# A graph layer on one core: VectorE's work kept behind each turning of edges, and more source rows fetched singly by SyncE

## The chip, the cores and the metric

The kernel runs on one core of a Trainium2 chip. The core has five engines that run at the same time, each with its own in-order queue: TensorE (PE; its weight loads are listed as PEld), VectorE (DVE), ScalarE (ACT), GpSimd (POOL) and SyncE (SP). Sixteen DMA engines move the data that these queues ask for. The metric is the time of one execution on the device in microseconds.

## The reference

One layer of a graph network on 8192 nodes with 256 channels and 131072 edges, sorted by their target node, all in float32:

```python
ea = edge_attr @ w_e + b_e                      # 131072 x 64 @ 64 x 256
msg = relu(x[src] + ea)                         # gather of source rows
agg = segment_sum(msg, dst, num_segments=8192)
t = x + agg
h_local = bn(relu(t @ w1 + b1) @ w2 + b2 + x)
# dense attention inside graphs of 32 nodes, 4 heads
h_attn = bn(attention(x) @ out_w.T + out_b + x)
out = h_local + h_attn
out = bn(out + relu(out @ m_w1 + m_b1) @ m_w2 + m_b2)
result = layernorm(x + out)
```

## The kernel before, in words

The edges are cut into 128 blocks of 1024. For each block:

- GpSimd gathers 1024 source rows into the tile xs by eight indirect DMAs of 128 rows (`gather`, L217). There are six xs buffers. Block 20 and later gather from xb, a copy of x with a bias added, that SyncE writes early on.
- SyncE loads the edge features of a pair of blocks into the tile ea by four DMAs of 256 KB (`load_edges`, L268). There are two ea buffers, a pair each.
- VectorE turns a block's features (`edge_transpose`, L288, a STREAM_TRANSPOSE eaT<-ea); there are two eaT buffers.
- TensorE multiplies them by the weights (`edge_products`, pe<-we,eaT). L174 is the line of a helper that issues nearly all matmuls.
- VectorE adds the products to the gathered rows (`edge_messages`, L348, xs<-pe,xs) and ScalarE takes the relu (L352).
- TensorE sums the messages by target (pw<-xs,oh, with oh built by VectorE's compares at L363), and later places the sums among the nodes of a chunk (l<-oh, and VectorE's xT<-l at L422).

Beside this runs all other work for sixteen chunks of 512 nodes: attention, then the dense layers. A chunk begins with the load of its nodes by ScalarE's queue (`load_nodes`, L428, xn<-in_x_dram, 512 KB) and ends with a store by SyncE (L749). In attention ScalarE copies the scores from PSUM (pr<-pe, L629) and VectorE turns them (bd<-pr, L649).

TensorE's order is written out by hand; VectorE's and ScalarE's too up to block 24 (NV). From there on a scheduler orders these two, with `tc.issue_after` keeping messages (L330) and compares (L359) behind the last turn. From block 104 (TAIL) on a planner sets the order, with `came` as the times at which blocks' rows are expected. GpSimd's gathers are held in step by `hold_fetches`: gather number n waits for a TensorE instruction of the written order whose modelled time is n × 1.254 − 10.

For the blocks in FETCHED the last of the eight gathers is left out, and SyncE fetches these 128 rows one by one into the tile xf (`row_stream`, L235 to L243): a step is one TENSOR_LOAD of sixteen addresses into SyncE's registers and sixteen DMAs of 1 KB, and eight steps make a block. `fetch_rows(b)` adds RUN to a quota for every block from FROM on; `some_rows` issues one step if the quota is 1 or more. It is called by `between()`, which is called after a block's messages. Their messages are three additions instead of one (L342): three quarters of the last pair from xs in two pieces, and the last quarter from xf.

SyncE's edge loads, rows and stores and ScalarE's xn loads share eight completion semaphores, handed out in turn in the order of the program. Each of these DMAs stands in its queue until the one that had its semaphore before has landed. So the rows behind four edge loads come to stand on them, and once per chunk a row of SyncE stands on ScalarE's xn load.

Of the kernel before, what the change touches and what calls it, by code (L numbers as in the profile page):

```python
# [12 lines left out]
AF = mybir.ActivationFunctionType  # L13
ALU = mybir.AluOpType
# [5 lines left out]
P = 128  # L20
N, C, E, ED, H, NPG = 8192, 256, 131072, 64, 4, 32
# [3 lines left out]
NB = E // BE  # L25
NH = 4
WN = P // NH
TJ = BE // NH // P
TB = NH * TJ
QR = 32  # L30
EQ = P // QR
# [7 lines left out]
GT = P // NPG  # L39
NX = 20  # L40
BUFS = 6
RUN = 0.75
RL = 4
FETCHED = [44, 54, 64, 76, 86, 98]
FROM = 26
ND = 2
NV = 24
TAIL = 104
# [36 lines left out]
def gnn_kernel(ctx: ExitStack, tc: tile.TileContext, x, src, dst, edge_attr, w, out):  # L85
    nc = tc.nc
# [16 lines left out]
    iota_n = const.tile([P, WB], FP, name="iota_n")  # L103
# [15 lines left out]
    rel = const.tile([P, NB, TB], FP, name="rel")  # L119
# [13 lines left out]
    r = 0  # L133
    for v in VECS:
        n = w[v].shape[0] // P
# [53 lines left out]
    def hold_fetches():  # L189
# [3 lines left out]
        for n, fetch in fetches:  # L193
# [8 lines left out]
            if i:  # L202
# [2 lines left out]
                    mybir.DependencyInfo(mybir.DependencyClass.Sync, mybir.DependencyReason.DATA), reason="hold",  # L205
                )

    def gather(b):
        xs = epool.tile([P, NH, TJ, C], FP, name="xs", tag="xs", bufs=BUFS)
        for h in range(NH):  # L210
            for j in range(TJ):
                if b in FETCHED and h * TJ + j == TB - 1:
                    continue
                idx = srcd[:, b * NH + h, j : j + 1] if b < ND else srci[:, b, h * TJ + j : h * TJ + j + 1]
                fetches.append((
                    b * TB + h * TJ + j,
                    nc.gpsimd.indirect_dma_start(  # L217
                        out=xs[:, h, j, :],
                        out_offset=None,
                        in_=x if b < NX else xb[:, :],  # L220
                        in_offset=bass.IndirectOffsetOnAxis(ap=idx, axis=0),
                    ).ins,
                ))
        xs_of[b] = xs

    last_src = const.tile([P, P], I32, name="last_src")
    xb_bytes = xb.rearrange("(o n) c -> o (n c)", o=1).bitcast(U8)
    xf_of = {}

    def row_stream():  # L230

        for b in FETCHED:
            xf = xf_of[b] = epool.tile([P, C], FP, name="xf", tag="xf", bufs=2)
            for r in range(0, QR, RL):
                _, rows = nc.values_load_multi_w_load_instructions(  # L235
                    last_src[b : b + 1, r * EQ : (r + RL) * EQ], engines=[mybir.EngineType.SP],
                    min_val=0, max_val=(N - 1) * C * 4,
                    skip_runtime_bounds_check_because="src holds rows of x, as for the gathers",
                )
                for i, at in enumerate(rows):  # L240
                    p = i % EQ * QR + r + i // EQ
                    nc.sync.dma_start(xf[p : p + 1, :].bitcast(U8), xb_bytes[:, ds(at, C * 4)])
                yield  # L243

    rows_to_come = row_stream()
# [2 lines left out]
    def fetch_rows(b):  # L248
        quota[0] += RUN if b >= FROM else 0

# [7 lines left out]
    def load_edges(b, n=2):  # L258
# [6 lines left out]
        for j in range(TJ):  # L265
            for i in range(ED // QR):
# [4 lines left out]
                )  # L271

    gather(0)
    gather(1)

    eaT_of, spots = {}, []
    stated = [True]

    def between():
        for do in spots:  # L280
            do()

    turned_at = [None]

    def edge_transpose(b):
        ea, g0 = ea_of[b // 2], b % 2 * NH * EQ
        eaT = eaT_of[b] = epool.tile([P, NH * EQ, QR], FP, name="eaT", tag="eaT", bufs=2)
        turned_at[0] = nc.vector.transpose(eaT, ea[:, QR:].rearrange("p (g d) -> p g d", d=ED)[:, g0 : g0 + NH * EQ, :QR]).ins  # L288


    pe_of, msg_of, oh_of, pw_of, newest = {}, {}, {}, {}, {}
# [30 lines left out]
    def edge_messages(b, pairs=range(0, NH, 2), of_pair=range(2)):  # L322

        xs = xs_of[b]
        if b not in msg_of:
            msg_of[b] = xs
        msg = msg_of[b]
        n = 2 if b < NB - 1 else 1
        with ExitStack() as behind:
            if not stated[0]:  # L330
                behind.enter_context(tc.issue_after(turned_at[0]))
            for h in pairs:
                pe = pe_of[b, h]
                for u in of_pair[::n]:
                    hs = slice(h + u, h + u + n)
                    if h + u + n == NH and b in FETCHED:
                        for us, js, rows in (
                            (slice(0, 2), slice(0, TJ - 1), xs[:, h:]), (slice(0, 1), slice(TJ - 1, TJ), xs[:, h:]),
                            (slice(1, 2), slice(TJ - 1, TJ), xf_of[b]),
                        ):  # L340
                            rows = rows[:, None, None, :] if rows is xf_of[b] else rows[:, us, js].rearrange("p u i c -> p i u c")
                            nc.vector.tensor_add(  # L342
                                msg[:, h:][:, us, js].rearrange("p u i c -> p i u c"), pe[:, js, us, :], rows
                            )
                        nc.scalar.activation(msg[:, hs], msg[:, hs], AF.Relu)
                        continue
                    for js in [slice(0, TJ)] if n == 2 or h + u < NH - 1 else [slice(j, j + 1) for j in range(TJ)]:
                        nc.vector.tensor_add(  # L348
                            msg[:, hs, js].rearrange("p u i c -> p i u c"), pe[:, js, u : u + n, :],
                            xs[:, hs, js].rearrange("p u i c -> p i u c"),  # L350
                        )
                        nc.scalar.activation(msg[:, hs, js], msg[:, hs, js], AF.Relu)  # L352
        between()

    def edge_hot(b):

        oh = oh_of[b] = epool.tile([P, TB, WN], FP, name="oh", tag="oh", bufs=2)
        with ExitStack() as behind:
            if not stated[0]:  # L359
                behind.enter_context(tc.issue_after(turned_at[0]))  # L360
            for t0 in range(0, TB, TB // 2):
                ts = slice(t0, t0 + TB // 2)
                nc.vector.tensor_tensor(  # L363
                    oh[:, ts],
                    iota_n[:, None, :WN].to_broadcast([P, TB // 2, WN]),
                    rel[:, b, ts, None].to_broadcast([P, TB // 2, WN]),
                    ALU.is_equal,
                )

    def group_sums(pw, i, b, turns):  # L370
        for h, j in turns:
# [58 lines left out]
    with tc.tile_pool(name="setup", bufs=1) as sp:  # L430
# [16 lines left out]
        for v in VECS:  # L447
            r, n = col[v]
# [14 lines left out]
        for b in range(2):  # L463
            edge_transpose(b)
            load_edges(b + 2)
# [86 lines left out]
        for h in range(1, NH):  # L552
            step = sp.tile([P, 1], FP, name="step", tag="step", bufs=2)
            nc.vector.tensor_scalar(step, iota_p, float(h * WN), float(-WN), ALU.is_ge, ALU.mult)
            nc.vector.tensor_add(iota_w, iota_w, step)
# [298 lines left out]
    class Work:  # L854
# [41 lines left out]
        def step(self, t, until):  # L896

            n = len(self.streams)
            for i in [k % n for k in range(self.turn, self.turn + n)]:
                while self.streams[i] and self.streams[i][0][0]() and t >= self.at[i]:  # L900
                    d = next(self.streams[i][0][1], None)
                    if d is None:
                        self.streams[i].pop(0)
                        self.at[i] = max(self.at[i], self.placed_at)
                    elif d == REST:
                        self.at[i] = t + 6.0
                    elif d > 0:
                        t += d
                        self.at[i], self.turn = t + 0.5, (i + 1) % n
                        return t  # L910
            later = [a for a, q in zip(self.at, self.streams) if q and q[0][0]() and a > t]
            return min([until, *later])
# [11 lines left out]
    with tc.manual_schedule(engines={PE}):  # L924
# [39 lines left out]
        for i, c, a, z in (  # L964
# [4 lines left out]
            if c < NCH - 1:  # L969
                d = dense(c * CH, chunk[c], npool, bank, a, z, *own)  # L970
            elif z < CH:
                d = dense_rows(c * CH, chunk[c], npool, bank, a, *own)
            else:
                d = last_part = dense_rows(c * CH, chunk[c], npool, lambda: next(last_banks), a, ahead=True)
# [10 lines left out]
        b = 0  # L985
        while b < TAIL:
# [24 lines left out]
            if stated[0]:  # L1011
# [8 lines left out]
                if waiting:  # L1020
                    pair_sums(1, waiting)
                    sums = edge_sums(waiting)
                waiting = list(blocks)
                edge_hot(b)
                edge_products(b + 1)
                edge_messages(b + 1)
# [32 lines left out]
            copy_some(4 * TN)  # L1059
            b += 2  # L1060

        came = [8.7 + 10.035 * (i + 1) for i in range(NB)]
        t, l, s = came[b - 2] + 20, b - 2, b - 2
        p, m = [b, 0], [b, 0]
        added = dict((i, came[i] + 2.0) for i in range(b))
# [9 lines left out]
        while l < NB:  # L1075
# [56 lines left out]
            elif t >= times[2]:  # L1132
                i, k = p
# [17 lines left out]
    with tc.If(wide > 0):  # L1151
        with tc.tile_pool(name="gen", bufs=1) as pool, tc.tile_pool(name="gen_ps", bufs=1, space=PSUM) as ps_pool:
# [11 lines left out]
            with tc.For_i(0, E, P * TE) as e0:  # L1164
                ea = pool.tile([P, TE, ED], FP, name="gea")
# [7 lines left out]
                xs = pool.tile([P, TE, C], FP, name="gxs")  # L1173
# [7 lines left out]
                for j in range(TE):  # L1181
# [4 lines left out]
                    pe = ps_pool.tile([P, C], FP, name="gpe", bufs=2)  # L1186
                    nc.tensor.matmul(pe, et, we[:ED, :], start=True, stop=True)
                    msg = pool.tile([P, C], FP, name="gmsg", bufs=2)
                    nc.vector.tensor_add(msg, pe, xs[:, j, :])
                    nc.scalar.activation(msg, msg, AF.Relu)  # L1190
                    d = df[:, j : j + 1]
# [79 lines left out]
```

## Time and profile before

| what | value |
|---|---|
| median of 3 runs | 1311.12 us (1310.87 to 1316.0) |
| profiled execution | 1310.63 us, span 1308.9 us |
| mean granted TensorE clock | 0.966 |
| gathers on GpSimd | 1018 |
| row DMAs on SyncE | 768, in 48 steps |
| edge loads on SyncE | 252 of 256 KB, 8 of 128 KB |
| VectorE's messages at L348 | 253 additions, 300.0 us |

The span is the time between the first and the last instruction that the profile has; the execution's own time is 1.73 us longer. All rows of the trace are in microseconds from the span's start. In a timeline's row the first number is the start, the second the time that the group of like instructions took, with their gaps; behind the operation stand output and inputs by the program's names, then how many there are, and in square brackets the idle time ahead of it and what ended it. SPq and ACTq are the queues in which SyncE and ScalarE issue DMAs.

### The profile page before, as it was taken

Reading aid. Unit: us, or ns where it says so; the run is one execution under the profiler, and the core shown is the slowest. Engines: PE = TensorE matmul, PEld = TensorE weight load, DVE = VectorE, ACT = ScalarE, POOL = GpSimd, SP = SyncE. Lnnn points to the kernel's source line nnn. Section 1 sums busy time; section 2 is a strip of 40 time slices with the busy share of each in tenths; the row PEclk is TensorE's granted clock in tenths of the full one; section 3 lists DMA queues with packets and bytes.
Section 4 is the critical chain, followed back from the end, with each engine's and each line's share of the span. In section 5 each row is a group of like instructions: output and inputs, shape, how many; then the busy total and the mean of one; then the engine's idle time right before and its main releaser. Section 6 shows DMA issues by size and latency. Waiting matters only on the chain.

```text
span 1308.9 us, 23368 instructions
## 1 busy us (share of the span) xinstructions
PE 1200.1 (92%) x7671; PEld 722.8 (55%) x7671; DVE 792.5 (61%) x1643; ACT 581.6 (44%) x840; POOL 971.1 (74%) x1026
## 2 busy tenths in 40 slices
PE   4997999899979989798998979979889999999997
PEld 3564556555546545555555545545455655556576
DVE  6676856647446565474746638346565765666563
ACT  3443534445526354352544426425245544545343
POOL 6777777777777777777777777777777777777772
PEclk9998999999999989899999989989989999999999
DMA  8999987767768657667687765866777775777642
GB/s 235 290 298 331 285 218 171 166 174 172 187 151 202 155 152 183 163 159 184 155 187 182 175 167 145 190 162 175 183 186 170 189 182 138 202 160 183 150 133 62
DMA packets 146298, 240.53 MB, mean 184 GB/s; under 512 B 24606, under 2 KB 109756, under 8 KB 145404
## 3 DMA queue, kind: packets, MB, share of 16 engines
q0 software_dynamic: 48864, 133.50, 38.1%
q1 hardware_dynamic: 88828, 98.15, 32.4%
q10 hardware_dynamic: 8480, 7.35, 1.9%
q8 instruction: 62, 1.02, 0.3%
q14 instruction: 64, 0.52, 0.1%
HBM read 222.13 MB, written 16.78 MB: 183 GB/s over the span
## 4 chain that ended last, share of the span: by engine, by line
PE 76%; DMA 9%; issue 5%; DVE 4%; POOL 3%; ACT 1%; SPq 0%; DVEq 0%; POOLq 0%; ACTq 0%
PE at L174 38%; PE pe L174 20%; PE pw L174 9%; PE l L174 5%; DMA xs<-xb,srci 4%; POOL xs L217 3%; DVE xs L348 2%; DMA xn<-in_x_dram 2%; DMA xs<-in_x_dram,srci 1%; PE at L775 1%; PE at L178 1%; DMA ea<-in_edge_attr_dram 1%; PE at L726 1%; ACT xs L352 1%; DMA last_src<-in_src_dram 0%
## 5 line engine op out<-in xcount | busy, mean ns | idle before, releaser
L217 POOL DMA_INDIRECT xs<-xb,srci x858 | 815.4, 950 | 262.3 <-issue 181.4
L352 ACT ACTIVATE xs<-xs 128x1024 f32<-128x1024 f32 (+2 forms) x253 | 263.0, 1045 | 434.0 <-DVE xs L348 357.8
L348 DVE TENSOR_TENSOR xs<-pe,xs 128x1024 f32<-128x1024 f32 (+2 forms) x253 | 300.0, 1204 | 211.1 <-PE pe L174 105.4
L174 PE MATMUL pe<-we,eaT 64*128 64x256 f32 x2048 | 271.1, 401 | 10.1 <-DVE xs L348 8.7
L174 PEld LDWEIGHTS pe<-we,eaT 64*128 64x128 f32 x2048 | 196.1, 194 | 108.5 <-issue 66.3
L174 PE MATMUL pw<-xs,oh 128*32 128x256 f32 x2048 | 142.9, 395 | 32.4 <-issue 20.2
L217 POOL DMA_INDIRECT xs<-in_x_dram,srci x144 | 138.6, 962 | 45.2 <-issue 29.3
L174 PEld LDWEIGHTS pw<-xs,oh 128*32 128x32 f32 x2048 | 61.0, 111 | 113.7 <-issue 54.1
L174 PE MATMUL at<-xT,inT 128*128 128x512 f32 x256 | 121.2, 600 | 1.9 <-ACT xT L578 1.9
L174 PE MATMUL at<-hA,mw 128*128 128x512 f32 (+1 forms) x256 | 114.4, 573 | 0.0
L288 DVE STREAM_TRANSPOSE eaT<-ea 128x512 f32<-128x512 f32 x128 | 89.6, 701 | 36.2 <-PE pe L174 31.4
L174 PE MATMUL at<-m,mw 128*128 128x512 f32 (+1 forms) x256 | 108.9, 570 | 0.0
L174 PEld LDWEIGHTS l<-oh,ws 128*128 128x128 f32 x512 | 74.7, 197 | 20.3 <-issue 16.4
L422 DVE TENSOR_TENSOR xT<-l,xT 128x352 f32<-128x352 f32 (+14 forms) x107 | 43.2, 427 | 70.4 <-PE l L174 70.3
L174 PE MATMUL l<-oh,ws 128*128 128x160 f32 (+4 forms) x512 | 85.8, 308 | 0.0
L174 PEld LDWEIGHTS at<-xT,inT 128*128 128x128 f32 x256 | 47.0, 190 | 60.5 <-issue 50.5
L174 PEld LDWEIGHTS at<-m,mw 128*128 128x128 f32 x256 | 47.0, 190 | 46.5 <-issue 42.2
L707 ACT ACTIVATE m<-at,vec 128x512 f32<-128x512 f32 (+1 forms) x64 | 41.8, 655 | 66.3 <-PE at L174 66.2
L174 PEld LDWEIGHTS at<-hA,mw 128*128 128x128 f32 x256 | 46.1, 190 | 44.0 <-issue 41.0
L591 ACT ACTIVATE qk<-at,vec 128x512 f32<-128x512 f32 x64 | 43.8, 685 | 52.9 <-PE at L174 52.5
L174 PE MATMUL pe<-qk 64*128 64x128 f32 x512 | 42.3, 321 | 23.2 <-DVE xs L348 23.2
L174 PE MATMUL at<-oT,outT 128*128 128x512 f32 x128 | 61.5, 604 | 0.3 <-ACT oT L664 0.3
(157 smaller groups left out, 1282.6 us busy)
## 6 DMA issues: line engine op xcount, KB each, us to landing
ea<-in_edge_attr_dram SPq DMA_DIRECT2D x252, 256.0 KB
xs<-xb,srci POOLq DMA_INDIRECT x858
xf<-xb SPq DMA_DIRECT2D x768, 1.0 KB
xn<-in_x_dram ACTq DMA_DIRECT2D x14, 512.0 KB
out_dram<-y SPq DMA_DIRECT2D x14, 512.0 KB
xp<-in_x_dram SPq DMA_DIRECT2D x10, 512.0 KB
xb<-xp SPq DMA_DIRECT2D x10, 512.0 KB
xp<-in_x_dram SPq DMA_DIRECT2D x3, 1024.0 KB
```

The source lines that it names most:

```text
L174: mark(ps, nc.tensor.matmul(ps, *args, **kw).ins)
L178: ins = nc.tensor.transpose(ps, *args).ins
L217: nc.gpsimd.indirect_dma_start(out=xs[:, h, j, :], out_offset=None, in_=x if b < NX else xb[:, :], in_offset=bass.IndirectOffsetOnAxis(ap= ...
L288: turned_at[0] = nc.vector.transpose(eaT, ea[:, QR:].rearrange("p (g d) -> p g d", d=ED)[:, g0 : g0 + NH * EQ, :QR]).ins
L348: nc.vector.tensor_add(msg[:, hs, js].rearrange("p u i c -> p i u c"), pe[:, js, u : u + n, :], xs[:, hs, js].rearrange("p u i c -> p i u c"),
L352: nc.scalar.activation(msg[:, hs, js], msg[:, hs, js], AF.Relu)
L422: newest["xT"] = nc.vector.tensor_add(xT, l2[:, :, a - n : z - n], xT).ins
L591: nc.scalar.activation(qk[:, o, :], ps, AF.Identity, bias=v_("in_b", o))
L707: newest["relu"] = nc.scalar.activation(m1[:, o, :], layer(mw1, KC, o, hA), AF.Relu, bias=v_("m_b1", o)).ins
L726: nc.tensor.transpose(ps[:wt, t - t2, k * P : (k + 1) * P], zT[:, k, t * P : t * P + wt], ident)
L775: nc.tensor.matmul(ps[i], wt[:, k, o * P : (o + 1) * P], act[:, k, :], start=(k == 0), stop=(k == nk - 1))
```

## The change

Three things are changed. FETCHED holds eleven blocks (36, 44, ..., 116) instead of six, and RUN and FROM are set so that each block brings one step. In the tail `skipped` takes the missing gathers out of the numbers that `hold_fetches` and `came` use, and `between()` is called there too. On VectorE, from block 24 on, every instruction that is written after a turn, and not only messages and compares, must be issued behind it; the two places in `edge_messages` and `edge_hot` that did this go. GpSimd has 1013 gathers, and SyncE 1408 row DMAs in 88 steps.

```diff
-RUN = 0.75
+RUN = 1
-FETCHED = [44, 54, 64, 76, 86, 98]
-FROM = 26
+FETCHED = list(range(36, 120, 8))
+FROM = 22
...
+    def skipped(b):
+        return sum(TAIL <= i <= b for i in FETCHED)
...
-                    b * TB + h * TJ + j,
+                    b * TB + h * TJ + j - skipped(b - 1),
...
-    turned_at = [None]
+    behind_turn = ctx.enter_context(ExitStack())
...
-        turned_at[0] = nc.vector.transpose(eaT, ...).ins
+        ins = nc.vector.transpose(eaT, ...).ins
+        behind_turn.close()
+        if not stated[0] and b < NB - 1:
+            behind_turn.enter_context(tc.issue_after(ins))
...
-        with ExitStack() as behind:
-            if not stated[0]:
-                behind.enter_context(tc.issue_after(turned_at[0]))
...
                         self.at[i], self.turn = t + 0.5, (i + 1) % n
+                        between()
                         return t
...
-        came = [8.7 + 10.035 * (i + 1) for i in range(NB)]
+        came = [8.7 + 10.035 * (i + 1) - 1.254 * skipped(i) for i in range(NB)]
```

SyncE's queue before, from the edge loads of blocks 50 and 51 (the first row) to the step behind those of blocks 54 and 55 (the last rows); last_src holds the source addresses, out_dram is the result:

```order
L268 DMA ea<-in_edge_attr_dram 32x8x256 x4
L235 TENSOR_LOAD last_src
L242 DMA xf<-xb 1x1024 x16
L749 DMA out_dram<-y 128x4x256
L268 DMA ea<-in_edge_attr_dram 32x8x256 x4
L235 TENSOR_LOAD last_src
L242 DMA xf<-xb 1x1024 x16
L235 TENSOR_LOAD last_src
L242 DMA xf<-xb 1x1024 x16
L268 DMA ea<-in_edge_attr_dram 32x8x256 x4
L235 TENSOR_LOAD last_src
L242 DMA xf<-xb 1x1024 x16
```

The same queue now, from the loads of blocks 50 and 51 (the first row) to those of blocks 54 and 55 (the last):

```order
L274 DMA ea<-in_edge_attr_dram 32x8x256 x4
L239 TENSOR_LOAD last_src
L246 DMA xf<-xb 1x1024 x16
L753 DMA out_dram<-y 128x4x256
L239 TENSOR_LOAD last_src
L246 DMA xf<-xb 1x1024 x16
L274 DMA ea<-in_edge_attr_dram 32x8x256 x4
L239 TENSOR_LOAD last_src
L246 DMA xf<-xb 1x1024 x16
L239 TENSOR_LOAD last_src
L246 DMA xf<-xb 1x1024 x16
L274 DMA ea<-in_edge_attr_dram 32x8x256 x4
```

Between two groups of edge loads stood one step and two steps by turns; now there are two steps each time, and the store stands between them.

VectorE before, at the turn of block 40 (third row); the messages in the last row are those of block 39, hA takes the results of attention and of the local branch, pr are scores, bd their block-diagonal form:

```order
L348 TENSOR_TENSOR xs<-pe,xs 128x2x2x256
L645 TENSOR_TENSOR pr<-pr,sm 128x128 x4
L288 STREAM_TRANSPOSE eaT<-ea 128x512
L649 STREAM_TRANSPOSE bd<-pr 32x16x32 x4
L701 SCALAR_TENSOR_TENSOR hA<-at,s_100,hA 128x512 x2
L363 TENSOR_TENSOR oh<-iota_n,rel 128x128 x2
L348 TENSOR_TENSOR xs<-pe,xs 128x2x2x256 x2
```

VectorE now, at the same turn (fourth row):

```order
L355 TENSOR_TENSOR xs<-pe,xs 128x2x2x256
L649 TENSOR_TENSOR pr<-pr,sm 128x128 x4
L653 STREAM_TRANSPOSE bd<-pr 32x16x32 x4
L294 STREAM_TRANSPOSE eaT<-ea 128x512
L705 SCALAR_TENSOR_TENSOR hA<-at,s_100,hA 128x512 x2
L367 TENSOR_TENSOR oh<-iota_n,rel 128x128 x2
L355 TENSOR_TENSOR xs<-pe,xs 128x2x2x256 x2
```

The four score turns moved from behind the edge turn to ahead of it; the messages behind it kept their place. Likewise, around the turn of block 78, before:

```order
L342 TENSOR_TENSOR xs<-pe,xf 128x256
L719 TENSOR_TENSOR zT<-at,zT 128x512
L288 STREAM_TRANSPOSE eaT<-ea 128x512
L363 TENSOR_TENSOR oh<-iota_n,rel 128x128 x2
L348 TENSOR_TENSOR xs<-pe,xs 128x2x2x256 x2
```

and now:

```order
L349 TENSOR_TENSOR xs<-pe,xf 128x256
L294 STREAM_TRANSPOSE eaT<-ea 128x512
L723 TENSOR_TENSOR zT<-at,zT 128x512
L367 TENSOR_TENSOR oh<-iota_n,rel 128x128 x2
L355 TENSOR_TENSOR xs<-pe,xs 128x2x2x256 x2
```

There the addition to zT (a dense layer's result) moved from ahead of the turn to behind it, still ahead of the messages of block 77.

More of the change, by code (lines that the diff above doesn't have):

```diff
@@ L227, in gnn_kernel @@
     xb_bytes = xb.rearrange("(o n) c -> o (n c)", o=1).bitcast(U8)
-    xf_of = {}
+    xf_of, all_of = {}, set()
     def row_stream():
@@ L242, in row_stream @@
                     nc.sync.dma_start(xf[p : p + 1, :].bitcast(U8), xb_bytes[:, ds(at, C * 4)])
+                if r + RL == QR:
+                    all_of.add(b)
                 yield
@@ L287, in edge_transpose @@
         eaT = eaT_of[b] = epool.tile([P, NH * EQ, QR], FP, name="eaT", tag="eaT", bufs=2)
-        turned_at[0] = nc.vector.transpose(eaT, ea[:, QR:].rearrange("p (g d) -> p g d", d=ED)[:, g0 : g0 + NH * EQ, :QR]).ins
+        ins = nc.vector.transpose(eaT, ea[:, QR:].rearrange("p (g d) -> p g d", d=ED)[:, g0 : g0 + NH * EQ, :QR]).ins
+        behind_turn.close()
+        if not stated[0] and b < NB - 1:
+            behind_turn.enter_context(tc.issue_after(ins))
     pe_of, msg_of, oh_of, pw_of, newest = {}, {}, {}, {}, {}
@@ L328, in edge_messages @@
         n = 2 if b < NB - 1 else 1
-        with ExitStack() as behind:
-            if not stated[0]:
-                behind.enter_context(tc.issue_after(turned_at[0]))
[L332 to L347, printed above, removed]
@@ new lines, in edge_messages @@
+        for h in pairs:
+            pe = pe_of[b, h]
+            for u in of_pair[::n]:
+                hs = slice(h + u, h + u + n)
+                if h + u + n == NH and b in FETCHED:
+                    assert b in all_of
+                    for us, js, rows in (
+                        (slice(0, 2), slice(0, TJ - 1), xs[:, h:]), (slice(0, 1), slice(TJ - 1, TJ), xs[:, h:]),
+                        (slice(1, 2), slice(TJ - 1, TJ), xf_of[b]),
+                    ):
+                        rows = rows[:, None, None, :] if rows is xf_of[b] else rows[:, us, js].rearrange("p u i c -> p i u c")
@@ L348, in edge_messages @@
                         nc.vector.tensor_add(
-                            msg[:, hs, js].rearrange("p u i c -> p i u c"), pe[:, js, u : u + n, :],
-                            xs[:, hs, js].rearrange("p u i c -> p i u c"),
-                        )
-                        nc.scalar.activation(msg[:, hs, js], msg[:, hs, js], AF.Relu)
+                            msg[:, h:][:, us, js].rearrange("p u i c -> p i u c"), pe[:, js, us, :], rows
+                        )
+                    nc.scalar.activation(msg[:, hs], msg[:, hs], AF.Relu)
@@ L353, in edge_messages @@
+                    continue
+                for js in [slice(0, TJ)] if n == 2 or h + u < NH - 1 else [slice(j, j + 1) for j in range(TJ)]:
+                    nc.vector.tensor_add(
+                        msg[:, hs, js].rearrange("p u i c -> p i u c"), pe[:, js, u : u + n, :],
+                        xs[:, hs, js].rearrange("p u i c -> p i u c"),
+                    )
+                    nc.scalar.activation(msg[:, hs, js], msg[:, hs, js], AF.Relu)
         between()
@@ L357, in edge_hot @@
         oh = oh_of[b] = epool.tile([P, TB, WN], FP, name="oh", tag="oh", bufs=2)
[L358 to L368, printed above, removed]
+        for t0 in range(0, TB, TB // 2):
+            ts = slice(t0, t0 + TB // 2)
+            nc.vector.tensor_tensor(
+                oh[:, ts],
+                iota_n[:, None, :WN].to_broadcast([P, TB // 2, WN]),
+                rel[:, b, ts, None].to_broadcast([P, TB // 2, WN]),
+                ALU.is_equal,
+            )
     def group_sums(pw, i, b, turns):
```

## The prediction

> **What bounds the kernel now.** I read the page's head first, then GpSimd's first and last gather on the timeline.
>
> ```profile
> span 1308.9 us, 23368 instructions
> PE 1200.1 (92%) x7671; PEld 722.8 (55%) x7671; DVE 792.5 (61%) x1643; ACT 581.6 (44%) x840; POOL 971.1 (74%) x1026
> ```
>
> ```profile
> 4.30 1.10 POOL L217 DMA_INDIRECT xs<-in_x_dram,srcd  x1 [2.70 <-issue]
> ...
> 1285.58 0.95 POOL L217 DMA_INDIRECT xs<-xb,srci  x1 [0.30 <-issue]
> ```
>
> TensorE is busiest by share, but GpSimd sets the pace. A gather takes 0.95 us and the next follows 0.30 us later, so neighbours start 1.25 us apart. The 1018 gathers start from 4.30 to 1285.58: 1017 distances of 1.26 us on average, so that they hardly ever stop. What follows the last one, 1308.9 − 1285.58 = 23.3 us, is the last block's way to the end. Whoever wants a shorter kernel must take gathers away, and this change takes away five.
>
> The other engine to look at is SyncE, which issues the rows that stand in for these gathers. Its waits from 470 to 960 us (us, times, longest), a row load's duration (min/median/max in ns), and its timeline over two pieces:
>
> ```profile
> SPq L242 <- DMA xn<-in_x_dram: 117.1, 6, 25.2
> SPq L242 <- DMA ea<-in_edge_attr_dram: 66.4, 55, 2.4
> L235 SPq TENSOR_LOAD <-last_src x48: 1159/1204/2488, 181.5 to 933.9; - x48
> ```
>
> ```profile
> 482.81 3.79 SPq L242 DMA_DIRECT2D xf<-xb  x12
> 486.70 2.58 SPq L268 DMA_DIRECT2D ea<-in_edge_attr_dram  x4
> ...
> 499.14 2.56 SPq L268 DMA_DIRECT2D ea<-in_edge_attr_dram  x4
> 503.07 16.67 SPq L242 DMA_DIRECT2D xf<-xb  x32
> 519.84 1.81 SPq L268 DMA_DIRECT2D ea<-in_edge_attr_dram  x4
> 522.98 8.26 SPq L242 DMA_DIRECT2D xf<-xb  x16
> 533.50 1.82 SPq L268 DMA_DIRECT2D ea<-in_edge_attr_dram  x4
> ```
>
> ```profile
> 804.17 10.31 SPq L242 DMA_DIRECT2D xf<-xb  x28
> 814.58 1.82 SPq L268 DMA_DIRECT2D ea<-in_edge_attr_dram  x4
> 817.75 8.51 SPq L242 DMA_DIRECT2D xf<-xb  x16
> 826.36 0.42 SPq L749 DMA_DIRECT2D out_dram<-y  x1
> 826.88 2.51 SPq L268 DMA_DIRECT2D ea<-in_edge_attr_dram  x4
> 831.02 16.58 SPq L242 DMA_DIRECT2D xf<-xb  x32
> 847.70 1.82 SPq L268 DMA_DIRECT2D ea<-in_edge_attr_dram  x4
> 850.84 8.30 SPq L242 DMA_DIRECT2D xf<-xb  x16
> 859.37 1.85 SPq L268 DMA_DIRECT2D ea<-in_edge_attr_dram  x4
> ```
>
> SyncE's queue is in order, and two things stop it there. Once per chunk of 512 nodes a row stands on the completion semaphore of ScalarE's xn load, six times for 117.1 us, 19.5 us each. And behind every group of edge loads some rows stand until these loads have landed. Twelve rows take 3.79 us, 0.32 us each; sixteen would take 5.1 but take 8.26 (522.98) or 8.30 (850.84). When only the last eight are left, some 8.9 us have passed since the first edge load was issued (522.98 + 8.26 − 2.5 − 519.84). So I take a pair's edge features to be there 8.9 us after their first issue.
>
> **Part by part: five gathers fewer.** 5 × 1.25 = 6.3 us, if GpSimd stays the bound. The span would be 1302.6 us. The profiled execution took 1310.63 us, 1.7 more than its span, and the median of the runs is 0.5 us above it: 1304.4 on this execution's own scale. That is 0.5% under the median, and 0.5% (6.6 us) is about what a measurement of this kernel can tell from no change.
>
> **The row fetches.** 640 rows in 40 more steps. A step is sixteen rows and one TENSOR_LOAD: 16 × 0.32 + 1.3 = 6.4 us, the 1.3 from the gap between 521.65 and 522.98. A pair of blocks had one and two steps by turns, and now has two each time, from block 36 to 114. The stores of finished chunks stand in the same queue and go out later, but nobody waits for them before the end. The pairs with one step cost 12.44, 13.66, 12.30 and 11.67 us from edge load to edge load (486.70, 519.84, 814.58, 847.70), 12.5 on average; with a second step I take 12.5 + 6.4 = 18.9. The pairs with two steps in the trace, both behind a store, cost 20.70 and 20.82 (499.14, 826.88); I take 20.8 for the one pair of four with a store, and keep 18.1 (11.67 + 6.4) and 20.8 as ends for all.
>
> Against SyncE's own sum this would still fit: two more steps per eight blocks are 12.8 us, and it stood 19.5 us on xn. But what counts is where it stands. Counting the DMAs in the changed program, the row that waits for xn stands nine rows ahead of the loads of blocks 40, 48, 56 and so on to 104, and ScalarE issues that xn load only behind work that needs the loads before. This closes a loop:
>
> ```profile
> 791.30 0.69 DVE L719 TENSOR_TENSOR zT<-at,zT 128x512 f32<-128x512 f32 x1 [3.44 <-PE at L174]
> 791.91 0.70 DVE L288 STREAM_TRANSPOSE eaT<-ea 128x512 f32<-128x512 f32 x1
> 792.90 2.35 DVE L348 TENSOR_TENSOR xs<-pe,xs 128x1024 f32<-128x1024 f32 x2
> ```
>
> ```profile
> 794.15 2.19 ACT L352 ACTIVATE xs<-xs 128x1024 f32<-128x1024 f32 x2 [4.84 <-DVE xs L348]
> 796.25 2.98 ACT L629 COPY pr<-pe 32x256 f32<-32x256 f32 x8
> 799.64 0.37 ACTq L428 DMA_DIRECT2D xn<-in_x_dram  x1
> ```
>
> These are an addition to zT, then VectorE's turn of block 78 and the messages of block 77 behind it, then ScalarE's relu of these messages, its copies of the attention scores and the xn load. From the turn to the xn load are 799.64 − 791.91 = 7.7 us, all in order; from there to SyncE's next row 804.17 − 799.64 = 4.5 us. One round of eight blocks, counted from the time at which SyncE goes on behind xn, is then:
>
> - nine rows, 2.9 us, to the loads of block 8k;
> - three pairs, 18.9 + 20.8 + 18.9 = 58.6 us, to the loads of 8k + 6;
> - 8.9 us to their landing and the turn of 8k + 6;
> - 7.7 us to the next xn load, 4.5 us to SyncE's row.
>
> Together 82.6 us. GpSimd needs 63 × 1.26 = 79.4 us for eight blocks, one of them with a fetched part. The loop is 3.2 us longer, and is the pace from the first xn on. In the kernel before the wait stood ahead of the loads of 8k + 2, so that two pairs with three steps lay between instead of three pairs with six: from 804.17 to the loads of block 86 at 847.70 it was 43.5 us, not 61.5.
>
> Where it begins:
>
> ```profile
> 399.25 0.38 ACTq L428 DMA_DIRECT2D xn<-in_x_dram  x1
> ```
>
> ```profile
> 373.33 1.81 SPq L268 DMA_DIRECT2D ea<-in_edge_attr_dram  x4
> ```
>
> ```profile
> 408.23 0.70 DVE L288 STREAM_TRANSPOSE eaT<-ea 128x512 f32<-128x512 f32 x1
> 408.86 2.81 DVE L649 STREAM_TRANSPOSE bd<-pr 32x512 f32<-32x512 f32 x4
> ...
> 413.43 2.35 DVE L348 TENSOR_TENSOR xs<-pe,xs 128x1024 f32<-128x1024 f32 x2
> ```
>
> The loads of blocks 40 and 41 went out at 373.33, long before the turn of block 40 at 408.23. Now they stand behind xn: 399.25 + 4.5 − 1.25 (one gather fewer by then) = 402.5, nine rows, 405.4, landed at 414.3. The turn is some 6 us late, and VectorE is in order: the messages of block 39 (413.43) are queued behind it, TensorE's window sums wait for these, and GpSimd for the buffers. Eight rounds on, SyncE goes on at 402.5 + 8 × 82.6 = 1063.3. The loads of block 114 are nine rows and five pairs further, 2.9 + 3 × 18.9 + 2 × 20.8 = 101.2: issued at 1164.5, landed at 1173.4.
>
> ```profile
> 1138.27 0.71 DVE L288 STREAM_TRANSPOSE eaT<-ea 128x512 f32<-128x512 f32 x1 [2.25 <-PE pe L174]
> ```
>
> ```profile
> 1120.00:1200.00 80.00, 79.76 (x506) 47.21 (x503) 51.32 (x105) 39.50 (x59) 60.74 (x64) 1.00 0.74 183
> ```
>
> The turn of block 114 was at 1138.27, so it is 35 us late. Nothing wins this back: in the stretch behind it (us, then busy us of PE, PEld, DVE, ACT, POOL) TensorE is busy for 79.76 of 80 us, and the work that is left there is the same. From 1138.27 to the end were 170.6 us: 1173.4 + 170.6 = 1344.0 for the span, and with 1.7 around it **1346 us**.
>
> The Trainium skill speaks against one term: "DMA: Bandwidth & Descriptors", section "Latency and other measured facts", gives a TENSOR_LOAD a floor of about 0.6 us. By that floor six steps in three pairs would be 4.2 us shorter and the round 78.4 us, under GpSimd's 79.4: no slowdown, the first rival's case. The trace has 1159 ns at the least, so the measurement decides.
>
> **The fetched blocks' additions.** Five more blocks have three additions at the end instead of one.
>
> ```profile
> L342 DVE TENSOR_TENSOR xs<-pe,xs x12: 354/544/692, 462.9 to 1008.0; 128x512 f32<-128x512 f32 x6, 128x256 f32<-128x256 f32 x6
> L342 DVE TENSOR_TENSOR xs<-pe,xf x6: 410/414/416, 463.9 to 1008.3; 128x256 f32<-128x256 f32 x6
> L348 DVE TENSOR_TENSOR xs<-pe,xs 128x1024 f32<-128x1024 f32 (+2 forms) x253 | 300.0, 1204 | 211.1 <-PE pe L174 105.4
> ```
>
> About 0.69 + 0.41 + 0.41 = 1.5 instead of 1.2 us, so 0.3 × 5 = 1.5 us in all, on an engine that is busy for 61%: nothing, or 1.5 us if the cover of the gathers is gone.
>
> **The barrier.** It lets no VectorE instruction written behind a turn pass ahead of it. The messages were bound in this way already; what changes sides are small pieces. At block 78 the zT addition, which sat 3.44 us on TensorE ahead of the turn, comes behind it: that turn is free up to 3.44 + 0.6 = 4 us earlier. At block 40 the four score turns, behind the turn before, come ahead of it: 2.8 us later. In both places the messages that follow stand behind turn and piece alike, before and after. The bounds, if one such piece per chunk were on the path over ten chunks, are −40 and +28 us; I take nothing, since the messages keep their place and VectorE has idle time (211.1 us ahead of the additions alone).
>
> **The rivals.** *GpSimd stays the bound* (not slower): the round stays under 79.4 us. For it speaks that SyncE's sum fits (19.5 against 12.8), and that with pairs at their lower end, 18.1 us, the round is 2.9 + 54.3 + 8.9 + 7.7 + 4.5 = 78.3. The point from which it decides is a mean pair of 18.5 us. Against it: the pairs with two steps that no xn wait cuts cost 20.7 and more. Then only the gathers count: 1304 us.
>
> *All pairs cost 20.8*: the round is 86.4 us, SyncE goes on at 1093.7, the loads of 114 have landed 2.9 + 104 + 8.9 later, 1209.5, and the end is at 1209.5 + 170.6 + 1.7 = 1382 us. For it: it is what such pairs cost in the trace. Against it: both stood behind a store, and three of four pairs will not.
>
> *The fetching doesn't bind, the barrier eats the gain*: half its upper bound, 14 us, less 6.3: about 1319; with a quarter about 1312. Against it: no row shows TensorE waiting for the moved pieces.
>
> **How the numbers follow.** The loop binds: 0.77, of which 0.12 near the heavy end. GpSimd stays the bound: 0.15; as its 1304.4 lies on the 0.5% line, it is half "faster", half "same". The barrier case: 0.08, most of it "same". So faster 0.08, same 0.13, slower 0.79. At the least round that binds, 79.4 us with pairs of 18.5 us, the same sum is 402.5 + 8 × 79.4 + 2.9 + 5 × 18.5 + 8.9 + 170.6 + 1.7 = 1314, at the heavy end 1382. The range, 1314 to 1385, takes in both and leaves the 1304 out.
>
> **What would show it.** Right: SyncE's rows standing on xn just ahead of the loads of every eighth block; VectorE idle ahead of the turns, put down to the edge loads, from block 40 on, for tens of us in all; gathers farther apart than 1.26 us from 410 to 1170; xn loads 82 to 83 us apart. Wrong: turns that find their edge features landed, xn loads 79 us apart, and an end some 23 us after the last gather near 1279.

## The result, and the profile after

The changed kernel takes 1370.28 us (median of 5 runs, 1367.82 to 1370.59) against 1311.12: a ratio of 1.0438 with an interval of 1.0421 to 1.0454, 59 us slower. The profiled execution has a span of 1366.0 us.

The head of its page, and the row of the turns from the groups (busy time and mean, then the idle time of VectorE just before them and what ended most of it):

```profile
span 1366.0 us, 24704 instructions
PE 1209.0 (89%) x7671; PEld 727.5 (53%) x7671; DVE 790.9 (58%) x1653; ACT 583.4 (43%) x840; POOL 967.2 (71%) x1021
L294 DVE STREAM_TRANSPOSE eaT<-ea 128x512 f32<-128x512 f32 x128 | 90.2, 706 | 294.1 <-DMA ea<-in_edge_attr_dram 251.2
```

The same row of the kernel before:

```profile
L288 DVE STREAM_TRANSPOSE eaT<-ea 128x512 f32<-128x512 f32 x128 | 89.6, 701 | 36.2 <-PE pe L174 31.4
```

No engine has more work to speak of: TensorE runs the same 7671 matmuls, though they keep it busy 8.9 us longer. VectorE, which turned edges as soon as TensorE left it a buffer, now sits 251.2 us ahead of the turns until edge features have landed. SyncE's timeline of the changed kernel over one round, from the loads of blocks 48 and 49 to those of 56 and 57 (the last row is the nine rows behind the xn wait, cut out of the 32 above it):

```profile
488.35 1.81 SPq L274 DMA_DIRECT2D ea<-in_edge_attr_dram  x4
491.53 15.31 SPq L246 DMA_DIRECT2D xf<-xb  x32
506.93 1.82 SPq L274 DMA_DIRECT2D ea<-in_edge_attr_dram  x4
510.13 8.70 SPq L246 DMA_DIRECT2D xf<-xb  x16
518.93 0.42 SPq L753 DMA_DIRECT2D out_dram<-y  x1
521.86 5.11 SPq L246 DMA_DIRECT2D xf<-xb  x16
527.07 1.81 SPq L274 DMA_DIRECT2D ea<-in_edge_attr_dram  x4
530.25 15.35 SPq L246 DMA_DIRECT2D xf<-xb  x32
545.70 1.81 SPq L274 DMA_DIRECT2D ea<-in_edge_attr_dram  x4
548.89 22.97 SPq L246 DMA_DIRECT2D xf<-xb  x32
571.95 1.82 SPq L274 DMA_DIRECT2D ea<-in_edge_attr_dram  x4
...
569.05 2.81 SPq L246 DMA_DIRECT2D xf<-xb  x9
```

And what follows the loads at 545.70 on VectorE and ScalarE:

```profile
554.53 0.71 DVE L294 STREAM_TRANSPOSE eaT<-ea 128x512 f32<-128x512 f32 x1 [8.36 <-DMA ea<-in_edge_attr_dram]
556.13 2.35 DVE L355 TENSOR_TENSOR xs<-pe,xs 128x1024 f32<-128x1024 f32 x2
...
565.14 0.37 ACTq L432 DMA_DIRECT2D xn<-in_x_dram  x1
```

This is the loop: loads at 545.70, the turn of block 54 at 554.53 the moment they are there, the xn load at 565.14, SyncE's rows again at 569.05, the next round's loads at 571.95. In the kernel before the loads of block 40 had gone out 35 us ahead of its turn (373.33 and 408.23); here a turn comes 9 us behind its loads.

The last gather starts at 1338.15, 52.6 us later than before.

The stretches towards the end show where time went on being lost (us, then busy us of PE, PEld, DVE, ACT, POOL); first the changed kernel, then the kernel before:

```profile
960.00:1040.00 80.00, 70.68 (x444) 41.56 (x446) 44.90 (x91) 34.72 (x48) 57.55 (x61) 0.98 0.69 168
1040.00:1120.00 80.00, 63.27 (x384) 36.99 (x376) 41.15 (x88) 32.83 (x47) 43.66 (x47) 0.87 0.62 146
1120.00:1200.00 80.00, 70.74 (x421) 40.76 (x421) 43.95 (x91) 32.17 (x50) 52.17 (x55) 0.96 0.68 162
```

```profile
960.00:1040.00 80.00, 78.52 (x518) 47.18 (x518) 53.77 (x110) 42.09 (x62) 60.31 (x65) 0.96 0.72 176
1040.00:1120.00 80.00, 76.24 (x511) 45.14 (x510) 54.85 (x117) 39.27 (x58) 60.50 (x65) 0.98 0.72 175
```

Before, TensorE was busy for 78.52, 76.24 and 79.76 of 80 us in these stretches; now for 70.68, 63.27 and 70.74. In these stretches alone it stood 29.8 us longer, and the stretch behind them wins nothing back (from 1200 to 1280 it was busy for 78.13 us before and for 76.16 now).

### The profile page after: what moved, and what is told of

It is laid out like the page before. It is cut to its first block, busy times and chain, and to the rows that moved or that the text cites. A ratio compares the mean times of both kernels' runs of the same rounds, so it can differ in the third digit from the quotient of the medians.

```text
span 1366.0 us, 24704 instructions
## 1 busy us (share of the span) xinstructions
PE 1209.0 (89%) x7671; PEld 727.5 (53%) x7671; DVE 790.9 (58%) x1653; ACT 583.4 (43%) x840; POOL 967.2 (71%) x1021
## 4 chain that ended last, share of the span: by engine, by line
PE 64%; DMA 15%; DVE 8%; issue 5%; ACT 4%; POOL 3%; SPq 2%; DVEq 0%; POOLq 0%; ACTq 0%
PE at L174 31%; PE pe L174 18%; PE pw L174 8%; DMA xs<-xb,srci 8%; PE l L174 4%; DVE xs L355 3%; POOL xs L221 3%; DMA ea<-in_edge_attr_dram 2%; DMA xs<-in_x_dram,srci 2%; DMA xn<-in_x_dram 1%; SPq L246 1%; PE at L178 1%; ACT xs L359 1%; PE at L779 1%; PE at L730 1%
## 5 line engine op out<-in xcount | busy, mean ns | idle before, releaser
L359 ACT ACTIVATE xs<-xs 128x1024 f32<-128x1024 f32 (+1 forms) x248 | 257.3, 1045 | 407.3 <-DVE xs L355 381.2
L355 DVE TENSOR_TENSOR xs<-pe,xs 128x1024 f32<-128x1024 f32 (+1 forms) x248 | 292.7, 1205 | 120.3 <-PE pe L174 77.6
L174 PE MATMUL pe<-we,eaT 64*128 64x256 f32 x2048 | 264.9, 394 | 16.3 <-DVE xs L355 15.5
L294 DVE STREAM_TRANSPOSE eaT<-ea 128x512 f32<-128x512 f32 x128 | 90.2, 706 | 294.1 <-DMA ea<-in_edge_attr_dram 251.2
L174 PEld LDWEIGHTS pe<-we,eaT 64*128 64x128 f32 x2048 | 192.5, 190 | 111.2 <-issue 68.3
L221 POOL DMA_INDIRECT xs<-in_x_dram,srci x144 | 139.3, 967 | 44.7 <-issue 29.8
L174 PE MATMUL pe<-qk 64*128 64x128 f32 x512 | 46.8, 348 | 52.1 <-DVE xs L355 52.1
L174 PEld LDWEIGHTS pe<-qk 64*128 64x128 f32 x512 | 42.4, 252 | 59.1 <-DVE xs L355 53.6
```

What stands on the lines that cost most here:

```text
L174: mark(ps, nc.tensor.matmul(ps, *args, **kw).ins)
L221: nc.gpsimd.indirect_dma_start(out=xs[:, h, j, :], out_offset=None, in_=x if b < NX else xb[:, :], in_offset=bass.IndirectOffsetOnAxis(ap= ...
L294: ins = nc.vector.transpose(eaT, ea[:, QR:].rearrange("p (g d) -> p g d", d=ED)[:, g0 : g0 + NH * EQ, :QR]).ins
L355: nc.vector.tensor_add(msg[:, hs, js].rearrange("p u i c -> p i u c"), pe[:, js, u : u + n, :], xs[:, hs, js].rearrange("p u i c -> p i u c"),
```

## The experiments

All kernels but the last group ran on chips on which the kernel before took 1312 us.

### The two halves of the change

The fetching alone (`fetch`, here against the changed kernel): the barrier goes, and messages and compares stand behind the last turn as before.

```diff
-    behind_turn = ctx.enter_context(ExitStack())
+    turned_at = [None]
...
+        with ExitStack() as behind:
+            if not stated[0]:
+                behind.enter_context(tc.issue_after(turned_at[0]))
```

> The eleven fetched blocks without the new barrier on VectorE (messages and compares alone stand behind the last turn, as before). Loop theory: SyncE's rows, edge loads and ScalarE's xn load stand in the same order as in the changed kernel but for one row, so the round of 82 to 83 us stays: 1366 to 1374 us. Rival, the barrier holds VectorE's small pieces and costs a part of the 59 us: clearly under 1360.

Measured: 1376.83 us, ratio 1.0476 (1.0447 to 1.0505). The fetching is the loss; without the barrier it is, if anything, a little worse.

The barrier alone (`barrier`):

```diff
-RUN = 1
-FETCHED = list(range(36, 120, 8))
-FROM = 22
+RUN = 0.75
+FETCHED = [44, 54, 64, 76, 86, 98]
+FROM = 26
```

> The new barrier alone, with the six fetched blocks and the rate of before. Loop theory: nothing of SyncE's order changes, GpSimd stays the bound: 1309 to 1313 us. Rival, the barrier costs by itself: 1315 to 1335 us, with VectorE idle ahead of turns or TensorE waiting for bd and hA.

Measured: 1321.42 us, ratio 1.0066 (1.0048 to 1.0084). This is the rival, if a small one: 9 us. TensorE's longest sums of waits from 960 us to the end (us, times, longest), for the barrier alone and then for the kernel before:

```profile
PE at L174 <- DVE bd L653: 8.5, 3, 5.9
PE pe L174 <- DVE xs L355: 6.7, 5, 2.8
```

```profile
PE pe L174 <- DVE xs L348: 6.5, 3, 3.5
...
PE at L174 <- DVE bd L649: 0.7, 1, 0.7
```

VectorE's timeline around the longest of these waits, at the turn of block 111, for the barrier alone and then for the kernel before (... where rows are left out):

```profile
1109.66 0.71 DVE L294 STREAM_TRANSPOSE eaT<-ea 128x512 f32<-128x512 f32 x1 [2.18 <-PE pe L174]
...
1111.04 2.35 DVE L355 TENSOR_TENSOR xs<-pe,xs 128x1024 f32<-128x1024 f32 x2
1113.30 0.68 DVE L639 TENSOR_REDUCE mx<-pr 128x16 f32<-128x512 f32 x1
...
1118.98 2.83 DVE L653 STREAM_TRANSPOSE bd<-pr 32x512 f32<-32x512 f32 x4
```

```profile
1104.27 0.69 DVE L635 TENSOR_REDUCE mx<-pr 128x16 f32<-128x512 f32 x1 [3.37 <-ACT pr L629]
...
1109.05 2.85 DVE L649 STREAM_TRANSPOSE bd<-pr 32x512 f32<-32x512 f32 x4
1111.93 0.71 DVE L288 STREAM_TRANSPOSE eaT<-ea 128x512 f32<-128x512 f32 x1
```

Before, a whole softmax of scores (mx, pr, sm, bd) ran ahead of the turn of block 111, most of it before TensorE had left the turn its buffer at 1108.65. With the barrier it stands behind that turn and its messages, bd is ready 10 us later, and TensorE waits 5.9 us for it; before, TensorE stood 2.7 us at this place, for messages. All the barrier's loss lies behind 960 us. Up to there TensorE is ahead with it: it runs 3244 matmuls from 400 to 960 us, against 3149 in the same order before. From 960 us to the end its waits add up to 21.0 us, against 10.0 before. That the order of the softmax pieces makes up all of this was not shown; the row of bd is 8.5 us of it.

### Cutting the loop

The xn loads issued by GpSimd (`xn_pool`), so that no row of SyncE stands on them:

```diff
-            load_nodes(n0, st, pool, nc.scalar)
+            load_nodes(n0, st, pool, nc.gpsimd)
```

> The changed kernel with the xn loads issued by GpSimd instead of ScalarE, so that no row of SyncE stands on them and the loop is cut; the rows stay. Loop theory: SyncE needs 3 x 18.9 + 20.8 = 77.5 us at most for eight blocks, under the 79.4 of the gathers, so the turns find their features; GpSimd pays some 14 x 1.3 us for the loads, and more where a load stands on its buffer: 1310 to 1335 us, nearly no VectorE idle time on edge loads. Rival, the rows by their number alone are too much for SyncE or for the DMA engines: 1365 us and more, VectorE idle on edge loads as in the changed kernel.

Measured: 1354.2 us, ratio 1.0316 (1.029 to 1.0343), 16 us better than the change and far from what the loop theory wanted. VectorE's row of the turns, and TensorE's longest sum of waits from 0 to 400 and from 960 to 1200:

```profile
L294 DVE STREAM_TRANSPOSE eaT<-ea 128x512 f32<-128x512 f32 x128 | 90.0, 704 | 53.7 <-PE pe L174 48.1
```

```profile
PE at L178 <- DMA xn<-in_x_dram: 22.6, 2, 16.5
...
PE at L178 <- DMA xn<-in_x_dram: 15.1, 3, 5.4
```

The waits for edge features are gone, so the loop is cut; but the cut has a price of its own. GpSimd's queue holds gathers back until TensorE has come to a mark, an xn load now stands behind such gathers, and TensorE waits for xn: 22.6 us ahead of 400 us, before any loop, and 15.1 us from 960 to 1200, where it waited 3.2 and 1.4 us in the changed kernel. The run shows that the rows fit, not what they cost without the loop.

The xn loads issued by SyncE itself (`xn_sync_again`): the load then stands beside the chunk's store, one pair ahead of the loads that the next turn of its kind needs, instead of three.

```diff
-            load_nodes(n0, st, pool, nc.scalar)
+            load_nodes(n0, st, pool, nc.sync)
```

> The changed kernel with the xn loads issued by SyncE, again, since the chip of the first run took 1599 us for the kernel before and TensorE bounded it there. Where the kernel before takes 1311 us, the loop theory says as then: no round of 82 us up to block 96 and turns at most 5 us later than before there, the losses behind block 100 stay: 1335 to 1352 us. Rival, the rows by their number: 1364 to 1375 us, VectorE idle on edge loads for 200 us and more.

Measured: 1322.78 us, ratio 1.0075 (1.005 to 1.01). All 1408 rows are there, and 48 of the 59 us are gone: more than the loop theory had asked for (1335 to 1352 us), and against the rival of the rows' number. The row of the turns, and SyncE's timeline over the same blocks as above:

```profile
L294 DVE STREAM_TRANSPOSE eaT<-ea 128x512 f32<-128x512 f32 x128 | 89.9, 703 | 47.7 <-PE pe L174 45.4
```

```profile
452.82 1.82 SPq L274 DMA_DIRECT2D ea<-in_edge_attr_dram  x4
...
484.93 0.41 SPq L432 DMA_DIRECT2D xn<-in_x_dram  x1
485.43 0.46 SPq L753 DMA_DIRECT2D out_dram<-y  x1
...
495.66 1.81 SPq L274 DMA_DIRECT2D ea<-in_edge_attr_dram  x4
...
514.09 1.83 SPq L274 DMA_DIRECT2D ea<-in_edge_attr_dram  x4
...
532.62 1.81 SPq L274 DMA_DIRECT2D ea<-in_edge_attr_dram  x4
```

The loads of block 48 go out at 452.82 instead of 488.35, the next round's at 532.62: 79.8 us apart, GpSimd's pace and not SyncE's. Hardly a turn waits for features (2.0 us in all). The losses behind block 100 shrank with the loop too, which neither theory had expected: most of them came with the late loads and not with the rows in the tail as such. What is left, some 10 us, is lost behind 960 us. Up to there TensorE is ahead of the kernel before (3247 matmuls from 400 to 960 us against 3149); from there on it waits for messages (9.4 us, 6.5 before), xn (7.9, none before), bd (2.9, 0.7 before) and xT (3.1, 2.1 before), and the five gathers bring nothing.

Without the barrier as well (`fetch_xn_sync_again`, the edits of `fetch` and `xn_sync_again` together):

> The eleven fetched blocks, xn loads on SyncE, no barrier, again, since the chip of the first run took 1603 us for the kernel before. Where the kernel before takes 1311 us: if the loop and the barrier are the two costs, the five gathers stay and the time is 1303 to 1310 us; rival, the rows cost something else that the barrier hid, 1316 to 1330 us.

Measured: 1326.8 us, ratio 1.011 (1.0093 to 1.0126). The rival again: with the loop and the barrier both gone the five gathers still don't show. TensorE's longest sums of waits from 960 us on:

```profile
PE pe L174 <- DVE xs L356: 10.0, 5, 3.6
PE at L178 <- DMA xn<-in_x_dram: 9.2, 3, 3.9
PE pw L174 <- ACT xs L360: 4.4, 2, 4.1
```

They add up to 23.6 us in these three rows; the same three were 6.8 us before. In the kernel before TensorE is busy nearly all the time from 960 us to 1280. This version, like the one with the barrier, lets it wait for xn, now late in SyncE's queue, and for messages. How much of the 15 us is the price of xn on SyncE and how much a cost of the rows in the tail stays open.

### A dose of the address loads

32 rows behind each TENSOR_LOAD instead of 16, half as many steps (`rl8`):

```diff
-RUN = 1
-RL = 4
+RUN = 0.5
+RL = 8
```

> The changed kernel with 32 rows behind each TENSOR_LOAD instead of 16, at half as many steps per block: the same 1408 rows, half the TENSOR_LOADs, and the row that stands on xn lies fourteen rows ahead of the loads of block 8k instead of eight. Loop theory: each pair is some 1.25 us shorter, so the round is 4.5 + (17.6 + 19.5 + 17.6) + 8.9 + 7.7 + 4.5 = 80.3 us, 0.9 instead of 3.2 over the pace of the gathers: 1315 to 1340 us, and xn loads some 80 us apart. Rival, it is the number of rows or the DMA engines' load and not the length of SyncE's way: 1360 to 1372 us.

Measured: 1364.74 us, ratio 1.0409 (1.0373 to 1.0444), whose interval overlaps that of the change: not the step that was expected, but inside the rival's 1360 to 1372 us. The load's row (min/median/max in ns) says why:

```profile
L239 SPq TENSOR_LOAD <-last_src x44: 2058/2112/2191, 183.7 to 1162.8; - x44
```

One load of 32 addresses takes 2112 ns, two of 16 take 2 x 1204: next to nothing is saved, 0.3 us for two steps and so 0.9 us for three pairs. From the loads of block 40 (404.35) to those of block 104 (1059.29) a round is 81.9 us, against 82.6 in the changed kernel. That agrees with the loop's sum, but a step so small tells hardly anything for the loop, and nothing against the rival.

### On slower chips

Six runs fell on two chips on which the kernel before took 1599 us (`to100`, `xn_sync`, `space10`, `fetch96`) and 1603 us (`fetch_xn_sync`, `before_xn_sync`). TensorE's busy time was 1326.3 us in the profile of `to100` and 1325.3 in that of `xn_sync`, instead of 1200.1. The balance of the engines is another one there, so they don't answer what they were made for. Two are kernels told above: `xn_sync` is that of `xn_sync_again`, and `fetch_xn_sync` that of `fetch_xn_sync_again`.

> The changed kernel with the xn loads issued by SyncE itself. They then stand beside the chunk's store, ahead of the loads of block 8k + 4, and wait there for their buffer; ScalarE's relu and score copies are no longer in the way from a turn to the next xn load, and one pair instead of three lies between the wait and the loads of 8k + 6. Loop theory: no round of 82 us up to block 96, turns at most 5 us later than before there; the losses behind block 100 stay: 1335 to 1352 us. Rival, the rows by their number: 1364 to 1375 us with VectorE idle on edge loads as in the changed kernel.

> The eleven fetched blocks with the xn loads on SyncE and without the barrier. If the two costs are the loop (gone with the xn loads on SyncE) and the barrier (1321 us alone), what stays are the five gathers: 1303 to 1310 us, and the version would beat both. Rival, SyncE's rows cost something else that the barrier's 9 us hid: 1316 to 1330 us.

The list cut at block 100 (`to100`, `FETCHED = list(range(36, 104, 8))`):

> The changed kernel with the list cut at block 100: nine fetched blocks (36, 44, ..., 100), no row in the stretch from block 102 on. It asks where the 59 us are lost. In the changed kernel ScalarE's thirteenth xn load is 20 us late (1057.97 against 1038.2), and the end 57 us. Loop theory with TensorE as the bound behind it: the 20 us of the rounds stay, the edge loads of the last blocks go out at once, and the 37 us that came later go but for the barrier's 9: 1330 to 1345 us. Rival, the loss behind block 100 comes with TensorE's new order or from late gathers whatever SyncE does: 1355 to 1372 us.

Every tenth block (`space10`, `FETCHED = list(range(36, 120, 10))`, `RUN = 0.8`), and the same cut at block 96 and without the barrier (`fetch96`, `range(36, 104, 10)`):

> The changed kernel with nine fetched blocks at every tenth (36, 46, ..., 116) and 0.8 of a step per block: a dose. Loop theory: three pairs have 4.8 steps on average instead of six, the round is 82.6 - 1.2 x 6.4 = 75 us, under the pace of the gathers, so the loop binds at most where three pairs with two steps follow each other; rows in the tail cost a part of their 28 us: 1312 to 1338 us. Rival, the cost goes with the number of rows (1152 against 768 and 1408): 1311 + 59 x 384/640 = 1346 us.

> The same dose without the barrier and with the list cut at block 96: seven fetched blocks (36, 46, ..., 96). If the loop, the rows in the tail and the barrier are all that costs, this is the kernel before with one gather fewer: 1307 to 1314 us. Rival, the row cost by number (896 against 768): 1320 us and more.

The kernel before with xn on SyncE (`before_xn_sync`):

> The kernel before with the xn loads on SyncE and nothing else. Loop theory: its round is not the pace there, so nothing is won: 1309 to 1314 us. Rival, xn on ScalarE costs the kernel before too, and the gain of 48 us on the changed kernel was partly that: under 1306 us.

Measured there, as ratios to the kernel before on the same chip: `to100` 1.0197 (1.0168 to 1.0226), `space10` 1.0144 (1.0111 to 1.0177), `fetch96` 1.0066 (1.0042 to 1.0091), `before_xn_sync` 0.9914 (0.9883 to 0.9944), and the two versions with xn on SyncE 1.0068 (1.0043 to 1.0092) with the barrier and 1.0072 (1.0044 to 1.0101) without. `before_xn_sync` is the only version of all that beat the kernel before, on its slower chip and by 0.9%; whether it does so on the faster ones wasn't measured. So a part of the 48 us that `xn_sync_again` got back may be what xn on SyncE brings to any version, and not the loop. Where a round has fewer steps it costs less there too, but a rate can't be read from it.

## Why the prediction was right

**The bound and the mechanism.** The loop was forecast as xn, rows, three pairs, landing, turn, xn. The trace has it, and `xn_sync_again`, which leaves every row and changes only where the xn load stands, takes VectorE's 251.2 us of waits for features down to 2.0 and gives 48 of the 59 us back. So the loop is shown as the cause of most of the loss, but for the part that xn on SyncE may bring by itself. That the rows' number isn't the cost is shown by the same run.

**The terms of the round**, for the round from 488.35 to 571.95:

| term | forecast | measured |
|---|---|---|
| three pairs | 58.6 | 545.70 − 488.35 = 57.4 |
| landing and turn | 8.9 | 554.53 − 545.70 = 8.8 |
| turn to xn load | 7.7 | 565.14 − 554.53 = 10.6 |
| xn load to SyncE's rows | 4.5 | 569.05 − 565.14 = 3.9 |
| nine rows | 2.9 | 571.95 − 569.05 = 2.9 |
| round | 82.6 | 83.6 |

The one term that was off, by 2.9 us, is the way from the turn to the xn load, and there the path itself was read wrongly. It was taken to end with ScalarE's score copies. But these end at 562.71, and the load goes out 2.4 us later, when VectorE has done the last additions that read the tile xn of an earlier chunk (y<-at,xn, 563.83 + 1.28 = 565.11):

```profile
561.23 1.48 ACT L633 COPY pr<-pe 32x256 f32<-32x256 f32 x4 [0.22 <-PE pe L174]
...
563.29 0.62 DVE L426 TENSOR_TENSOR xT<-l,xT 128x448 f32<-128x448 f32 x1 [3.76 <-PE l L174]
563.83 1.28 DVE L736 TENSOR_TENSOR y<-at,xn 128x512 f32<-128x512 f32 x2
```

These additions stand in VectorE's queue behind the turn, its messages and a wait of 3.76 us for TensorE, so the loop closes all the same. In all eight rounds the load goes out within 0.05 us of their end. At the place where the prediction read its 7.7 us it was the same, but there the copies ended only 0.4 us earlier, so that the time fitted:

```profile
798.33 1.28 DVE L732 TENSOR_TENSOR y<-at,xn 128x512 f32<-128x512 f32 x2
```

Over eight rounds SyncE's loads of block 40 and block 104 stand like this:

```profile
404.59 1.83 SPq L274 DMA_DIRECT2D ea<-in_edge_attr_dram  x4
...
1065.31 1.82 SPq L274 DMA_DIRECT2D ea<-in_edge_attr_dram  x4
```

That is 660.7 us, 82.6 a round, as forecast; the loads of block 104 were forecast for 1063.3 + 2.9 = 1066.2. Up to here the sum holds within a microsecond. Some of that is luck: over the eight rounds the way from the turn to the xn load took 9.6 us on average (8.9 to 10.6) instead of 7.7, and three pairs 56.9 us (55.7 to 58.1) instead of 58.6, and the two errors cancel. The floor of 0.6 us for a TENSOR_LOAD, from the Trainium skill's "DMA: Bandwidth & Descriptors", section "Latency and other measured facts", was reached in no row shown here: 1159 ns at the least for 16 addresses, 2058 for 32.

**The end was mis-sized**: 1346 was forecast, 1370 measured. Two terms. From the loads of block 104 to the turn of block 114 five pairs without an xn wait and a landing were taken, 1173.4 − 1066.2 = 107.2 us. But the rows of the last pair stood 17.5 us on one more xn load, so that this pair took 32.8 us, and the turn came at 1181.4, after 116.1 us:

```profile
1142.99 29.55 SPq L246 DMA_DIRECT2D xf<-xb  x32
1172.64 1.81 SPq L274 DMA_DIRECT2D ea<-in_edge_attr_dram  x4
...
1181.40 0.71 DVE L294 STREAM_TRANSPOSE eaT<-ea 128x512 f32<-128x512 f32 x1 [3.14 <-DMA ea<-in_edge_attr_dram]
```

And from there 170.6 us were taken as a full TensorE; it took 184.6, since TensorE didn't stay full. Together with a start 0.9 us early these make up the 22.0 us by which the span was longer than forecast. "Nothing wins this back" was right; that more could be lost was not thought of.

**The barrier at nothing** was wrong by itself, +9 us within bounds of −40 and +28. The step that failed is "the messages keep their place": the softmax pieces don't, and in the last stretch what waits for them is TensorE. With eleven fetched blocks the barrier was no loss: 1.0438 with it and 1.0476 without, 1.0075 and 1.011 with the loop cut.

**Rivals.** "GpSimd stays the bound, 1304" didn't come true even with the loop cut. It had taken 23.3 us behind the last gather as given, but TensorE is nearly full from 960 us on even in the kernel before, and the lead that the versions with xn on SyncE have at 960 us is lost behind it. How many of the five gathers would show without these waits stays open.

## What to carry to other kernels

When work is added to an in-order queue that has time to spare by its sum, look for what it waits on and follow that back, link by link, to what really ends each wait: if the way leads through other engines to the queue's own earlier work, the sum of the loop decides and not the queue's total. A wait between two queues through shared completion semaphores is such an edge, and moving one load to another place can cut it. Before counting on fewer instructions of the pacing engine, look whether another one is full in the last stretch: savings end there.

## What was not expected of the hardware

A TENSOR_LOAD's time goes with the number of addresses: 1204 ns for 16 and 2112 ns for 32. And the kernel before took 1311 to 1312 us on some chips and 1599 and 1603 us on two others, with GpSimd's gathers as short as before (953 ns against 950 in `to100`) and TensorE's granted clock at 0.91 instead of 0.97 in the profile of `to100`. There TensorE's busy time is 10.5% longer and the clock 6% lower, while the kernel before takes 22% longer; so the clock explains a part of that at most, and the rest stays open.
